# A two-layer graph network: a planner's due times set by pair, and its choice between two kinds of matmul

## Chip, cores, metric

One NeuronCore of one Trainium2 chip runs the whole program. The metric is device time in microseconds of one execution; the kernel before takes 771.95 us (median of three runs, 770.51 to 772.46). TensorE is the matmul engine (PE in profiles, PEld its weight loads), VectorE is DVE, ScalarE is ACT, GpSimd is POOL, SyncE is SP.

## What is computed

128 graphs of 128 nodes with 64 features go through two layers, each with a residual and a layer norm. `x` is (128, 128, 64), `adj` is (128, 128, 128), symmetric in its pattern, about 6% of its entries are nonzero, the diagonal included.

```python
# layer 0
mask = (adj > 0.0)
xj_proj = x @ W1a
diff = x[:, :, None, :] - x[:, None, :, :]
h = relu(xj_proj[:, :, None, :] + diff @ W1b + b1)
hm = einsum('bjkh,bjk->bjh', h, mask)
y = hm @ W2 + deg[..., None] * b2
x = layernorm(x + y)
# layer 1
agg = einsum('bmn,bnd->bmd', adj, x)
h = elu(agg @ V1 + c1)
h = elu(h @ V2 + c2)
x = layernorm(x + h @ V3 + c3)
```

## The kernel before, in words

Two graphs make a pair, and 64 pairs go through a software pipeline. Layer 0 would need a hidden vector for each of 128 x 128 node pairs; the kernel makes one only for edges. Nodes are sorted by degree, each sorted node gets as many slots as its place may need, and the slots of a pair are cut into nine blocks (`BLOCKS`: first node, last node, slots a node). A block is a *unit*. For each unit ScalarE copies the nodes' own part into a PSUM bank (L839), TensorE adds the neighbours' part by 18 matmuls against a one-hot matrix (L851, `oh`), and VectorE sums absolute values over the slots (L860, `sums`). There are four such banks (`edges`, `NE = 4`), so a unit's copy waits for the reduction of the unit four before.

Around the units each pair has these stages, written as generators that yield one step at a time:

- `prepare`: degrees (L532, VectorE), keys (L539, L540, POOL), their spread over the partitions (L545, L547, TensorE), ranks and permutation (L554, L561, VectorE).
- `sort_x` and `project_a`: L574, L578, L582, then L592 (TensorE, three matmuls), the bias copies L599 that make `aj`, `sa` (L606, POOL), L612 and L615, `ea` (L621) and `corr` (L628).
- `sort_mask`: L637, L640 (TensorE), copies L645 and L647, L651 (TensorE), `vp` (L654), and nine one-hot blocks (L661, VectorE).
- `turn` and `project_c`: transposes L676, L677 with copy L681, then L694, L697 (TensorE) and the split of their result into three bf16 parts `cp` (L704, L708, L711, L713).
- `finish`: `hm` (L771, POOL), L776, L780, L783 (TensorE), `ys` (L787), L793 (TensorE), the first norm, L800 and L809 (TensorE), an ELU (`r` L755, `e` L758, `h` L761), L815, a second ELU, L820 and L822, the second norm, the output (L826, an SP DMA).

The matmuls of the units and L578, L612, L615, L800 produce 64 output partitions each, and two of them run in the two column halves of the array (128*64 in the profile); the kernel calls this mode `PE:t`. All others use the full array (128*128; L694 two row halves, 64*128), mode `PE`.

The order on each engine is not written by hand. `Flow` (L88 to L174) plans it while the program is built: a simulated clock for each engine, a list of threads (generators), each with a next step that has an engine, a cost, the events it needs and a due time. `run` finds the step that can start first, then looks at the steps on the same engine that could start within `NEAR` (for TensorE `NEAR_PE`) of it, and takes the one with the lowest rank. The rank is the due time, plus `HOLD` if the step would change TensorE's mode; a change also delays a step by `SWITCH` in the plan. The due times are the tables `DUE`, one figure a step, plus `ROUND` times the pair's number; a unit's is `pace(u)`, and a unit's copy isn't planned before that. A step's result counts as there `LAG` after its planned end. The chip sees only the order; semaphores that follow from it do the rest, and no clock is waited for on the chip. Loads of pair p + 3 start with the first unit of pair p (`AHEAD`).

Of the kernel before, what the change touches and what calls it, by code (L numbers as in the profile page):

```python
# [87 lines left out]
class Flow:  # L88
# [8 lines left out]

    LAG = 0.2
    NEAR = 0.1
    NEAR_PE = 0.03  # L100
    SWITCH = 0.1
    HOLD = 0

    def __init__(self, banks):
        self.clock = {}
# [41 lines left out]
    def _switch(self, engine, mode):  # L147
        return self.SWITCH if engine == "PE" and mode != self.mode else 0.0

    def _rank(self, th):  # L150
        engine, _, mode = th[4][0].partition(":")
        return th[0] + (self.HOLD if self._switch(engine, mode) else 0.0), th[1]

    def run(self):
        while self.threads:
            ready = [(t, th) for t, th in ((self._ready(th[4]), th) for th in self.threads)
                     if t is not None]
            t, th = min(ready, key=lambda r: (r[0], r[1][0], r[1][1]))
            first = th[4][0].split()[0].partition(":")[0]
            near = t + (self.NEAR_PE if first == "PE" else self.NEAR)  # L160
            t, th = min((r for r in ready if r[1][4][0].split()[0].partition(":")[0] == first
                         and r[0] <= near), key=lambda r: self._rank(r[1]))
            engine, cost, after, banks, fn = th[4]
            args = []
            if banks:
                self.free.sort(key=lambda f: f[0])
                args = [self.free.pop(0)[1] for _ in range(banks)]
            fn(*args)
            for e in engine.split():
                e, _, mode = e.partition(":")  # L170
                self.clock[e] = t + cost
                if e == "PE":
                    self.mode = mode
            self._next(th, ([t + cost + self.LAG], *args))  # L174


def sparse(tc, env):
# [4 lines left out]
    LAY, NB = g.LAY, g.NB  # L182
# [6 lines left out]
    EV = {}  # L189


    ROUND = 11.14
    AHEAD = 3
    PACE = ROUND / NB

    DUE = {
        "prepare": (-34.32, -34.43, -29.25, -33.33, -26.26),
        "sort_x": (-25.05, -19.47, -20.79, -15.63, -11.78, -14.33, -11.15, -5.27, -5.97),
        "sort_mask": (-24.98, -24.21, -19.11, -17.63, -31.08, -14.67, -12.13, -9.2, -7.19, -6.42,
                      -4.21, -1.99, -12.24, -7.24),  # L200
        "turn": (-25.52, -21.42),
        "project_c": (-19.53, -25.02, -26.5, -19.03, -18.18, -16.73, -23.86),
        "finish": (7.83, 15.84, 19.72, 16.78, 21.09, 22.6, 28.99, 31.57, 29.07, 31.37, 30.6,
                   34.42, 35.7, 33.91, 37.94, 41.34, 41.72, 43.55, 44, 37.02, 51.36),
        "unit": (-1.1, 0.98, 2.36),
    }

    def pace(u):
        return PACE * u

    def begin_thread(name, p, gen):
        flow.start(ROUND * p, DUE[name], gen)
# [310 lines left out]
    def prepare(p):  # L523

        a = ADJ[p]
        d = S[p] = {}
        mk = d["mk"] = prep.tile([P, 2, N], BF16, name="mk")
        deg = prep.tile([P, 2], F32, name="deg")

        def count():  # L530
            for s in range(2):
                nc.vector.tensor_scalar(mk[:, s, :], a[:, s, :], 0.0, 0.0, op0=OP.is_gt,  # L532
                                        op1=OP.add, accum_out=deg[:, s:s + 1])
        ev, = yield ("DVE", 0.54, [event("load", p)], 0, count)
        degb = prep.tile([P, 2], BF16, name="degb")
        keyc = prep.tile([P, 2], F32, name="keyc")

        def keys():
            nc.gpsimd.tensor_copy(degb, deg)  # L539
            nc.gpsimd.tensor_sub(keyc, deg, jcol)  # L540
        ev, = yield ("POOL PORT", 0.43, [ev] + made("jcol"), 0, keys)

        def spread(key):
            for s in range(2):
                nc.tensor.matmul(key[:, s * N:(s + 1) * N], degb[:, s:s + 1].to_broadcast([P, P]),  # L545
                                 identb, start=True, stop=True)
            nc.tensor.matmul(key[:, 2 * N:3 * N], small, iotb, start=True, stop=True)  # L547
        ev, key = yield ("PE", 0.17, [ev] + made("identb", "small", "iotb"), 1, spread)
        pos = prep.tile([P, 2], F32, name="pos")
        cmp = prep.tile([P, 2, N], BF16, name="cmp", bufs=3)  # L550

        def rank():
            for s in range(2):
                nc.vector.scalar_tensor_tensor(cmp[:, s, :], key[:, s * N:(s + 1) * N],  # L554
                                               keyc[:, s:s + 1], tie, op0=OP.subtract,
                                               op1=OP.is_gt, accum_out=pos[:, s:s + 1])
        ev, = yield ("DVE", 0.54, [ev] + made("tie"), 0, rank)
        permb = d["permb"] = prep.tile([P, 2, N], BF16, name="permb")

        def permute():  # L560
            nc.vector.tensor_tensor(permb, key[:, 2 * N:3 * N].rearrange("p (s n) -> p s n", s=1)  # L561
                                    .to_broadcast([P, 2, N]),
                                    pos.rearrange("p (s o) -> p s o", o=1).to_broadcast([P, 2, N]),
                                    op=OP.is_equal)
        ev, = yield ("DVE", 0.36, [ev], 0, permute)
        flow.give(key, ev)
        begin_thread("sort_x", p, sort_x(p, ev))
        begin_thread("sort_mask", p, sort_mask(p, ev))
# [17 lines left out]
    def project_a(p, xsT, ev):  # L586
# [16 lines left out]
        happened(ev, "aj", p)  # L603
        have = ev
        sa = prep.tile([P, 3, N], F32, name="sa", bufs=3)
        evs, = yield ("POOL PORT", 0.95, [have] + made("srow"), 0, lambda: nc.gpsimd.tensor_mul(sa, aj, srow))  # L606

        def short(eb):

# [60 lines left out]
    def turn(p):  # L670
# [3 lines left out]
        def transpose(t):  # L674
            for s in range(2):
                nc.tensor.transpose(t[:, s * N:(s + 1) * N], a[:, s, :], ident)  # L676
            nc.tensor.transpose(t[:, 2 * N:3 * N], flat(xx), ident)  # L677
        ev, t = yield ("PE", 0.4, [event("load", p)] + made("ident"), 1, transpose)
        turned = d["turned"] = prep.tile([P, 3, N], F32, name="turned", bufs=9)
        ev, = yield ("ACT", act(3 * N), [ev], 0,  # L680
                     lambda: nc.scalar.copy(flat(turned), t[:, :3 * N]))  # L681
# [34 lines left out]
    def norm(yps, ev, name, rest, shift):  # L716
# [15 lines left out]
        def factors():  # L732
            nc.gpsimd.tensor_scalar(ve, st[:, :, 2], 1.0 / F, EPS, op0=OP.mult, op1=OP.add)  # L733
            nc.gpsimd.tensor_tensor(rs, ve, mhalf, op=OP.pow)  # L734
            if shift:
                for s in range(2):
                    nc.gpsimd.tensor_scalar(nb[:, s:s + 1], st[:, s, 1:2], rs[:, s:s + 1], -1.0,  # L737
                                            op0=OP.mult, op1=OP.mult)
        ev, = yield ("POOL PORT", 1.24 if shift else 0.88, [ev] + made("mhalf"), 0, factors)
        o = work.tile([P, 2, F], F32, name=name, bufs=6)  # L740

        def apply():
# [23 lines left out]
    def finish(p):  # L766
# [24 lines left out]
        def unsort(t):  # L791
            for s in range(2):
                nc.tensor.matmul(t[:, s * O:(s + 1) * O], d["permT"][:, s, :],  # L793
                                 ys[:, s * O:(s + 1) * O], start=True, stop=True)
        ev, t = yield ("PE", 0.45, [ev, event("permT", p)], 1, unsort)
        x1, ev = yield from norm(t, ev, "x1", xx, True)

        def aggregate(t):
# [8 lines left out]
        def hidden1(zb):  # L807
            for s in range(2):
                nc.tensor.matmul(zb[:, s * N:(s + 1) * N], v1p[:, s, :], agg,  # L809
                                 start=True, stop=True)  # L810
        ev, zb = yield ("PE", 0.45, [ev] + made("v1p"), 1, hidden1)
        h1, ev = yield from elu(zb, ev, "h1", 0)

        def hidden2(zb):
            nc.tensor.matmul(zb[:, :2 * N], v2s, h1, start=True, stop=True)  # L815
        ev, zb = yield ("PE", 0.44, [ev], 1, hidden2)
        h2, ev = yield from elu(zb, ev, "h2", 1)

        def last(t):
# [300 lines left out]
```

## Time and profile before

| | us |
|---|---|
| median of three runs | 771.95 |
| profiled execution | 770.88 |
| its span, first to last instruction | 769.0 |
| first L851 matmul starts at | 22.8 |
| L851: busy TensorE time, 10368 matmuls | 390.6 |
| L860: busy VectorE time, 576 reductions | 330.2 |
| L839: busy ScalarE time, 576 copies | 309.7 |
| L661: busy VectorE time, 576 blocks | 167.6 |

The clock that TensorE was granted is 0.994 over the span. Busy times are sums over the profiled execution; records of TensorE overlap, since one matmul's end runs beside the next one's start. An fp32 matmul appears as two records. Matmul lines show the array's shape in use behind the tile names (128*64, 128*128, 64*128), then the moving operand. In a timeline, equal instructions that follow each other are one line: start, time from first start to last end, and their number.

### The profile page before, as it was taken

To read this page: it belongs to the slowest core of one execution; us is meant where nothing else is said; L and a number is where in the kernel's file an instruction comes from. 1 tells how busy PE (TensorE), PEld (TensorE's weight loads), DVE (VectorE), ACT (ScalarE), POOL (GpSimd) and SP (SyncE) were. 2 spreads that over 40 slices of the span, in tenths; PEclk is the share of its full clock that TensorE was granted. 3 is DMA by queue.
4 is the path that set the end of the run, shared out by engine and by line. 5 is a ranking of instruction groups with operands and counts; after the bars stand their busy time and mean duration, and the time that the engine had idled before them with its cause. 6 is when DMAs were issued, how large, how long until landed. Compare 5 with 4: busy or idle time off the path is not lost.

```text
span 769.0 us, 35363 instructions
## 1 busy us (share of the span) xinstructions
PE 746.9 (97%) x14487; PEld 671.7 (87%) x14488; DVE 717.1 (93%) x2357; ACT 702.0 (91%) x1990; POOL 432.9 (56%) x806
## 2 busy tenths in 40 slices
PE   7899999999999999999999999999999999999993
PEld 5688998999899899889889889989899889989992
DVE  7999999999999999999999999999999999999982
ACT  5788999999999999999999999999999999999974
POOL 6445565665665665655555555556566566566542
PEclk9999999999999999999999999999999999999997
DMA  3011110110111011011011011011011011100000
GB/s 81 3 24 26 27 30 21 27 31 20 27 30 27 21 30 30 16 31 30 18 30 31 17 30 30 21 27 30 21 27 30 21 27 30 27 20 21 10 9 18
DMA packets 63881, 19.75 MB, mean 26 GB/s; under 512 B 46816, under 2 KB 63712, under 8 KB 63712
## 3 DMA queue, kind: packets, MB, share of 16 engines
q1 hardware_dynamic: 63008, 17.12, 9.6%
q8 instruction: 115, 1.88, 1.1%
q14 instruction: 54, 0.44, 0.2%
q10 hardware_dynamic: 704, 0.30, 0.2%
HBM read 13.14 MB, written 4.19 MB: 23 GB/s over the span
## 4 chain that ended last, share of the span: by engine, by line
PE 93%; DVE 3%; ACT 1%; DMA 1%; issue 1%; POOL 0%; ACTq 0%; DVEq 0%
PE e L851 44%; PE m L592 6%; PE m L776 5%; PE m L694 5%; PE m L809 4%; PE m L815 4%; PE m L822 4%; PE m L793 3%; PE m L578 2%; PE m L676 2%; PE m L800 2%; PE m L637 2%; PE m L651 2%; PE m L780 1%; PE m L697 1%; DVE sums L860 1%
## 5 line engine op out<-in xcount | busy, mean ns | idle before, releaser
L851 PE MATMUL e<-oh,cp 128*64 128x162 bf16 (+3 forms) x10368 | 390.6, 228 | 1.8 <-ACT e L839 1.5
L851 PEld LDWEIGHTS <-cp 128*64 128x64 bf16 x10368 | 356.8, 110 | 30.6 <-issue 22.6
L860 DVE TENSOR_REDUCE sums<-e 128x54 f32<-128x486 f32 (+8 forms) x576 | 330.2, 608 | 12.8 <-PE e L851 12.4
L839 ACT COPY e<-aj 128x504 f32<-128x504 f32 (+6 forms) x576 | 309.7, 558 | 7.2 <-DVE sums L860 6.7
L661 DVE TENSOR_TENSOR oh<-vp,slotc 128x336 bf16<-128x336 bf16 (+6 forms) x576 | 167.6, 319 | 1.8 <-PE e L851 1.7
L606 POOL TENSOR_TENSOR sa<-aj,srow 128x384 f32<-128x384 f32 x64 | 65.3, 1020 | 121.6 <-ACT aj L599 118.8
L733 POOL TENSOR_SCALAR ve<-st 128x2 f32<-128x2 f32 x128 | 24.5, 191 | 156.1 <-DVE st L726 150.5
L734 POOL TENSOR_TENSOR rs<-ve,mhalf 128x2 f32<-128x2 f32 x128 | 88.9, 695 | 10.6
L713 POOL TENSOR_TENSOR cp<-r,cp 128x512 bf16<-128x512 f32 x64 | 74.2, 1159 | 13.2 <-ACT cp L711 13.2
L771 POOL TENSOR_TENSOR hm<-sums,corr 128x384 f32<-128x384 f32 x64 | 64.0, 1000 | 11.8 <-DVE sums L860 11.8
L755 ACT ACTIVATE r<-m,cc 128x256 f32<-128x256 f32 x128 | 64.3, 502 | 4.1 <-PE m L809 3.1
L628 POOL TENSOR_TENSOR corr<-ea,sa 128x384 f32<-128x384 f32 x64 | 64.1, 1001 | 0.9 <-DVE ea L621 0.7
L761 DVE SCALAR_TENSOR_TENSOR h<-m,cc,e 128x256 f32<-128x256 f32 x128 | 60.7, 475 | 3.7 <-ACT e L758 3.7
L592 PE MATMUL m<-xsT,wad 128*128 128x128 f32 x384 | 58.3, 288 | 0.8 <-DVE r L708 0.6
L599 ACT ACTIVATE aj<-m,b1c 128x128 f32<-128x128 f32 x192 | 57.0, 375 | 1.0 <-PE m L592 1.0
L744 ACT ACTIVATE x<-y,nb,rs 128x64 f32<-128x64 f32 x128 | 49.4, 434 | 9.3 <-POOL nb L737 9.2
L758 ACT ACTIVATE e<-r 128x256 f32<-128x256 f32 x128 | 57.6, 451 | 0.1
L554 DVE SCALAR_TENSOR_TENSOR cmp<-m,keyc,tie 128x128 bf16<-128x128 f32 x128 | 39.9, 349 | 16.3 <-PE m L547 15.4
L776 PE MATMUL m<-w2d,hm 128*128 128x128 f32 x384 | 53.9, 277 | 0.3 <-POOL hm L771 0.3
L708 DVE TENSOR_TENSOR r<-m,cp 128x256 f32<-128x256 f32 x128 | 52.2, 411 | 0.8 <-ACT cp L704 0.7
L776 PEld LDWEIGHTS m<-w2d,hm 128*128 128x128 f32 x384 | 48.6, 193 | 1.0 <-POOL hm L771 0.5
L592 PEld LDWEIGHTS m<-xsT,wad 128*128 128x128 f32 x384 | 47.7, 191 | 1.8 <-DVE r L708 0.8
(145 smaller groups left out, 1346.8 us busy)
## 6 DMA issues: line engine op xcount, KB each, us to landing
adj<-in_adj_dram SPq DMA_DIRECT2D x64, 128.0 KB, 2.4
xx<-in_x_dram SPq DMA_DIRECT2D x64, 64.0 KB, 2.3
out_dram<-o SPq DMA_DIRECT2D x64, 64.0 KB, 1.7
degs<-ys SPq DMA_DIRECT2D x64, 1.0 KB, 1.7
w1s<-in_L_gnn_W_dram ACTq DMA_DIRECT2D x2, 96.0 KB, 3.1
w2s<-in_L_gnn_W_dram ACTq DMA_DIRECT2D x2, 48.0 KB, 2.8
v2s<-in_L_gnn_W_dram SPq DMA_DIRECT2D x1, 64.0 KB, 3.0
v1d<-in_L_gnn_W_dram SPq DMA_DIRECT2D x2, 32.0 KB, 2.0
```

The lines of the kernel that those rows point to most:

```text
L592: nc.tensor.matmul(aps[:, c * N:(c + 1) * N], wad[:, c, :], xsT, start=True, stop=True)
L606: evs, = yield ("POOL PORT", 0.95, [have] + made("srow"), 0, lambda: nc.gpsimd.tensor_mul(sa, aj, srow))
L628: ev, = yield ("POOL PORT", 1.05, [ev, evs], 0, lambda: nc.gpsimd.tensor_sub(corr, ea, sa))
L661: lambda: nc.vector.tensor_tensor(oh[:, :, c].rearrange("p b (s w) -> p b s w", w=w), vp[:, :, p0:p1].rearrange("p b (o w) -> p b o w", o= ...
L713: lambda: nc.gpsimd.tensor_sub(cp[:, 2], r1, cp[:, 1]))
L734: nc.gpsimd.tensor_tensor(rs, ve, mhalf, op=OP.pow)
L755: lambda: nc.scalar.activation(r, z, AF.Relu, bias=c, scale=-1.0))
L771: lambda: nc.gpsimd.tensor_sub(hm, d["sums"], d["corr"]))
L776: nc.tensor.matmul(yb[:, :2 * O], hm[:, c, :], flat(w2d[:, c]), start=(c == 0), stop=False)
L839: lambda: nc.scalar.copy(e.rearrange("p (c s w) -> p c s w", c=3, w=w), d["aj"][:, :, p0:p1].rearrange("p c (o w) -> p c o w", o=1) .to_br ...
L851: nc.tensor.matmul(e[s * HB:(s + 1) * HB, c * n:(c + 1) * n], cp[:, k, s, c * HB:(c + 1) * HB], oh[:, s, base:base + n], start=False, stop ...
L860: nc.vector.tensor_reduce(d["sums"][:, :, p0:p1], e.rearrange("p (c s w) -> p c w s", c=3, w=w), AX.X, OP.add, apply_absolute_value=True)
```

## The change

No tile, matmul, copy or DMA is changed; the diff is to what the planner is told.

- `NEAR_PE` goes from 0.03 to 0.05. A new `STAY` of 0.1 lets a TensorE step of the mode now in use be chosen if it could start within 0.1 of the earliest. `HOLD` goes from 0 to 9.1, so among the steps in reach one that changes the mode ranks as if due 9.1 us later.
- `ROUND` goes from 11.14 to 10.91. A unit's `pace` was spread evenly, `ROUND / 9` apart; it is now `ROUND` times the pair plus 0.59 times the unit's number, so the nine are due within 4.7 us of their pair's start.
- All tables of `DUE` are new. Preparing steps are due later than before (the first of `prepare` at -21.43 instead of -34.32), finishing steps earlier (the last used ones around 20 instead of 37 to 51).
- Planned costs of seven steps change by 0.03 to 0.11 either way.

```diff
@@ -97,9 +97,10 @@
 
     LAG = 0.2
     NEAR = 0.1
-    NEAR_PE = 0.03
+    NEAR_PE = 0.05
     SWITCH = 0.1
-    HOLD = 0
+    STAY = 0.1
+    HOLD = 9.1
 
     def __init__(self, banks):
         self.clock = {}
@@ -147,6 +148,9 @@
     def _switch(self, engine, mode):
         return self.SWITCH if engine == "PE" and mode != self.mode else 0.0
 
+    def _same(self, th):
+        return th[4][0].split()[0].partition(":")[2] == self.mode
+
     def _rank(self, th):
         engine, _, mode = th[4][0].partition(":")
         return th[0] + (self.HOLD if self._switch(engine, mode) else 0.0), th[1]
@@ -158,8 +162,11 @@
             t, th = min(ready, key=lambda r: (r[0], r[1][0], r[1][1]))
             first = th[4][0].split()[0].partition(":")[0]
             near = t + (self.NEAR_PE if first == "PE" else self.NEAR)
+
+            stay = t + self.STAY if first == "PE" else near
             t, th = min((r for r in ready if r[1][4][0].split()[0].partition(":")[0] == first
-                         and r[0] <= near), key=lambda r: self._rank(r[1]))
+                         and (r[0] <= near or r[0] <= stay and self._same(r[1]))),
+                        key=lambda r: self._rank(r[1]))
             engine, cost, after, banks, fn = th[4]
             args = []
             if banks:
@@ -189,24 +196,24 @@
     EV = {}
 
 
-    ROUND = 11.14
+    ROUND = 10.91
     AHEAD = 3
-    PACE = ROUND / NB
+    UNIT = 0.59
 
     DUE = {
-        "prepare": (-34.32, -34.43, -29.25, -33.33, -26.26),
-        "sort_x": (-25.05, -19.47, -20.79, -15.63, -11.78, -14.33, -11.15, -5.27, -5.97),
-        "sort_mask": (-24.98, -24.21, -19.11, -17.63, -31.08, -14.67, -12.13, -9.2, -7.19, -6.42,
-                      -4.21, -1.99, -12.24, -7.24),
-        "turn": (-25.52, -21.42),
-        "project_c": (-19.53, -25.02, -26.5, -19.03, -18.18, -16.73, -23.86),
-        "finish": (7.83, 15.84, 19.72, 16.78, 21.09, 22.6, 28.99, 31.57, 29.07, 31.37, 30.6,
-                   34.42, 35.7, 33.91, 37.94, 41.34, 41.72, 43.55, 44, 37.02, 51.36),
-        "unit": (-1.1, 0.98, 2.36),
+        "prepare": (-21.43, -22.36, -22.69, -20.72, -21.04),
+        "sort_x": (-15.03, -12.06, -13.19, -6.77, -6.47, -11.28, -12.01, 0.14, 0.41),
+        "sort_mask": (-12.71, -9.98, -12.21, -12.26, -12.11, -7.07, -6.36, -6.41, -5.45, -4.29,
+                      -4.35, -3.8, -3.8, -4.28),
+        "turn": (-16.08, -7.32),
+        "project_c": (-14.14, -13.31, -10.75, -12.7, -10.78, -6.83, -12.64),
+        "finish": (-0.94, 6.84, 5.02, 8.44, 9.21, 9.24, 8.9, 10.51, 16.67, 19.63, 14.77, 10.14,
+                   15.75, 12.69, 17.93, 20.46, 19.2, 19.6, 23.98, 19.96, 19.4, 20.24, 21.31),
+        "unit": (1.9, 2.36, 3.81),
     }
 
     def pace(u):
-        return PACE * u
+        return ROUND * (u // NB) + UNIT * (u % NB)
 
     def begin_thread(name, p, gen):
         flow.start(ROUND * p, DUE[name], gen)
@@ -538,7 +545,7 @@
         def keys():
             nc.gpsimd.tensor_copy(degb, deg)
             nc.gpsimd.tensor_sub(keyc, deg, jcol)
-        ev, = yield ("POOL PORT", 0.43, [ev] + made("jcol"), 0, keys)
+        ev, = yield ("POOL PORT", 0.32, [ev] + made("jcol"), 0, keys)
 
         def spread(key):
             for s in range(2):
@@ -603,7 +610,7 @@
         happened(ev, "aj", p)
         have = ev
         sa = prep.tile([P, 3, N], F32, name="sa", bufs=3)
-        evs, = yield ("POOL PORT", 0.95, [have] + made("srow"), 0, lambda: nc.gpsimd.tensor_mul(sa, aj, srow))
+        evs, = yield ("POOL PORT", 1.0, [have] + made("srow"), 0, lambda: nc.gpsimd.tensor_mul(sa, aj, srow))
 
         def short(eb):
 
@@ -675,7 +682,7 @@
             for s in range(2):
                 nc.tensor.transpose(t[:, s * N:(s + 1) * N], a[:, s, :], ident)
             nc.tensor.transpose(t[:, 2 * N:3 * N], flat(xx), ident)
-        ev, t = yield ("PE", 0.4, [event("load", p)] + made("ident"), 1, transpose)
+        ev, t = yield ("PE", 0.33, [event("load", p)] + made("ident"), 1, transpose)
         turned = d["turned"] = prep.tile([P, 3, N], F32, name="turned", bufs=9)
         ev, = yield ("ACT", act(3 * N), [ev], 0,
                      lambda: nc.scalar.copy(flat(turned), t[:, :3 * N]))
@@ -736,7 +743,7 @@
                 for s in range(2):
                     nc.gpsimd.tensor_scalar(nb[:, s:s + 1], st[:, s, 1:2], rs[:, s:s + 1], -1.0,
                                             op0=OP.mult, op1=OP.mult)
-        ev, = yield ("POOL PORT", 1.24 if shift else 0.88, [ev] + made("mhalf"), 0, factors)
+        ev, = yield ("POOL PORT", 1.27 if shift else 0.97, [ev] + made("mhalf"), 0, factors)
         o = work.tile([P, 2, F], F32, name=name, bufs=6)
 
         def apply():
@@ -792,7 +799,7 @@
             for s in range(2):
                 nc.tensor.matmul(t[:, s * O:(s + 1) * O], d["permT"][:, s, :],
                                  ys[:, s * O:(s + 1) * O], start=True, stop=True)
-        ev, t = yield ("PE", 0.45, [ev, event("permT", p)], 1, unsort)
+        ev, t = yield ("PE", 0.4, [ev, event("permT", p)], 1, unsort)
         x1, ev = yield from norm(t, ev, "x1", xx, True)
 
         def aggregate(t):
@@ -808,12 +815,12 @@
             for s in range(2):
                 nc.tensor.matmul(zb[:, s * N:(s + 1) * N], v1p[:, s, :], agg,
                                  start=True, stop=True)
-        ev, zb = yield ("PE", 0.45, [ev] + made("v1p"), 1, hidden1)
+        ev, zb = yield ("PE", 0.49, [ev] + made("v1p"), 1, hidden1)
         h1, ev = yield from elu(zb, ev, "h1", 0)
 
         def hidden2(zb):
             nc.tensor.matmul(zb[:, :2 * N], v2s, h1, start=True, stop=True)
-        ev, zb = yield ("PE", 0.44, [ev], 1, hidden2)
+        ev, zb = yield ("PE", 0.48, [ev], 1, hidden2)
         h2, ev = yield from elu(zb, ev, "h2", 1)
 
         def last(t):
```

## Prediction

> **What bounds the kernel now.** I read the shares of busy time first, then the busy time of the engines in single rounds (a round is one pair of graphs: nine units plus all other stages of one pair each), then the waits, then TensorE's own timeline inside a round.
>
> ```profile
> PE 746.9 (97%) x14487; PEld 671.7 (87%) x14488; DVE 717.1 (93%) x2357; ACT 702.0 (91%) x1990; POOL 432.9 (56%) x806
> PE 93%; DVE 3%; ACT 1%; DMA 1%; issue 1%; POOL 0%; ACTq 0%; DVEq 0%
> ```
>
> TensorE is the chain that ended last for 93% of the span. A busy TensorE is not yet a bound, so the rounds have to confirm it; columns are stretch, then length, then PE, PEld, DVE, ACT and POOL busy, then clock and DMA:
>
> ```profile
> 22.80:34.00 11.20, 10.27 (x234) 8.68 (x234) 10.51 (x31) 8.60 (x24) 4.30 (x4) 1.00 0.01 2
> 300.00:311.43 11.43, 11.43 (x230) 10.38 (x230) 10.96 (x37) 10.90 (x32) 6.62 (x12) 1.00 0.11 27
> 500.00:511.43 11.43, 11.43 (x228) 10.37 (x227) 10.96 (x37) 10.89 (x33) 6.62 (x12) 1.00 0.11 26
> 746.10:769.00 22.90, 9.98 (x77) 7.60 (x71) 7.98 (x24) 9.07 (x27) 7.30 (x17) 0.80 0.07 15
> ```
>
> The timeline repeats every 11.43 us, and in such a round TensorE is busy throughout, VectorE 10.96 and ScalarE 10.90. The view of TensorE's waits between 100 and 700 us is empty: no matmul there waits for another engine. So a round costs what its matmuls cost one after the other, and VectorE and ScalarE have about half a microsecond left. In the last 22.9 us TensorE works less than half the time: there the end of the last pair is a chain of latencies.
>
> What is inside TensorE's 11.43 us is seen where its array changes between column halves (128*64, units and L578, L612, L615, L800) and the full array (128*128). The start of a group minus the start of the one before is what that one cost:
>
> ```profile
> 302.36 0.50 PE L851 MATMUL e<-oh,cp 128*64 128x154 bf16 x9
> ...
> 302.78 0.28 PE L651 MATMUL m<-mtp,prefix 128*128 128x256 bf16 x1
> 302.90 0.83 PE L776 MATMUL m<-w2d,hm 128*128 128x128 f32 x6
> 303.57 0.34 PE L780 MATMUL m<-cp,mtp 128*128 128x64 bf16 x6
> ...
> 305.44 0.50 PE L809 MATMUL m<-agg,v1p 128*128 128x128 f32 x3
> 305.87 0.34 PE L851 MATMUL e<-oh,cp 128*64 128x170 bf16 x4
> ...
> 309.33 0.61 PE L822 MATMUL m<-v3s,h 128*128 128x64 f32 x4
> 309.87 0.70 PE L694 MATMUL m<-wc,turned 64*128 64x256 f32 x4
> ...
> 732.07 0.61 PE L822 MATMUL m<-v3s,h 128*128 128x64 f32 x4
> 732.52 0.89 PE L776 MATMUL m<-w2d,hm 128*128 128x128 f32 x6
> 733.24 0.34 PE L780 MATMUL m<-cp,mtp 128*128 128x64 bf16 x6
> ```
>
> Six L776 records take 303.57 - 302.90 = 0.67, 0.112 each. Three L809 records of the same shape, up to a unit, take 305.87 - 305.44 = 0.43 instead of 0.336: 0.09 more. The other way, nine unit records before L651 take 0.42, while unit records of this size run at 36 in 1.28 (299.89 to 301.17), 0.32 for nine: 0.10 more. L822 before L694, which uses row halves, takes 0.54 for four records; the same four before L776, where the shape stays, take 732.52 - 732.07 = 0.45, so 0.09 more. So each change of the array's shape costs about 0.10 us, in either direction and for a shape the planner does not distinguish.
>
> **What the skill says.** The Trainium skill, "TensorEngine Tiling (Array Packing)", Key Properties: "Changing tiling mode (not just tile) drains the TensorE." It gives no price; the trace agrees and gives 0.09 to 0.10. "TensorE: Matmul & The Clock Gate", Weight-path perf modes: fast weight load is not on for fp32 weights. The trace agrees: L776's fp32 records load for 193 ns (PEld row) and L822's 64-column records still cost 0.11 each (0.45 for four), as much as 128 columns; so an fp32 group that follows a very short matmul pays for its first load (L592, behind the one-column L783, takes 304.55 - 303.80 = 0.75 for six, 0.08 over L776). The same page, Part 2: only TensorE's loads are pulled ahead, its matmuls stay in program order. So the order as built is the order that runs.
>
> **The change, part by part.**
>
> 1. No instruction of computation is added, removed or resized. Due times, costs and the three constants are read only by the planner, so the effect is the new order, and the waits that follow from it.
>
> 2. Changes of shape. From the built order I counted, between full-array and column-half work: before, 278 in all, and from round 7 on exactly four in each round (two full-size runs per pair). After, 382 in all, and from round 7 to 61, 55 rounds, six in each: units 154, 170, 162 / L809, L651 / units 66, 168 / L776 to L783, L815, L694, L697, L793 / units 112, 168, 154, 169 / L820, L822, L592, L676, L677, L637, L640, L545, L547. The short run L809 + L651, about half a microsecond of work, stands alone. So the new order has three full-size runs per pair where the old one has two, whatever HOLD is meant to do. L694's own two changes to row halves stay inside a full-size run in both. Startup has ten fewer (33 for 43), the end four more; the sum is +104. At 0.105 each (0.09 to 0.10 measured at the boundary, plus about 0.02 because the first unit behind a change starts slower: the 170-unit takes 305.87 to 306.55, 0.68, for 0.66 at the pace of the units behind it, in half of the changes): +10.9 us. Bounds 104 x 0.09 = +9.4 and 104 x 0.12 = +12.5.
>
> 3. First fp32 loads. Before, a round pays L592 behind L783 0.08, L809 behind the 64-column L793 0.05 and L815 behind L547 about 0.05 (0.58 for two double-width records, less 0.45 and the change's 0.09): 0.18. After, L815 stands behind L783 (0.08), L793 behind the 64-column bf16 L697 (0.05), and L592 behind L822 (0.05: at 732.52 the six L776 behind L822 take 0.72, against 0.67). L809 and L776 now open full-size runs, which only bf16 groups do before; the end shows what an fp32 group pays there: L793 behind a unit takes 0.50 for four (731.02 to 731.52), 0.05 over L822's 0.45. With 0.05 each the new sum is 0.28. Net +0.10 a round, times 55: +5.5 us, bounds 0 and +10.
>
> 4. Start and end. Work is also moved across the ends. Before, behind the last unit stand six L809, eight L822, three L815 and four L793 instructions; after, four, six, two and two. One pair's worth of each, about 0.45 us a group, hence 1.8 us, ran in an end in which TensorE idles and now runs in rounds that it bounds: +1.8. Ahead of the first unit two pairs' L592 (1.5 us) and some L637, L651 and L545 are gone (0.7): the first unit may start about two microseconds sooner, and the work comes back in the early rounds; in the stretches from 22.8 to 34 us TensorE idles 0.9, so part is absorbed, but less prepared work also means early units that wait. I take +1 for it, bounds -3 (all early idling filled) and +6. The latency chain of the last pair, from its last unit to its output, is the same operations: 0.
>
> 5. Waits in a round. Every engine queue was reordered and the planner now sets more semaphore waits (290 more instructions that only wait, some three a round on TensorE, one each on VectorE and POOL). In the trace such a wait on TensorE takes 0.05 in its queue ahead of the array (not in its busy time), with matmuls running: 0, unless what it waits for is late. The tightest of the new places is L815 behind L809: unit 66, its reduction on VectorE, the two L532 counts, h (L761), then L815. From the unit's start: unit 0.28, matmul end 0.19, reduction 0.35, counts 2 x 0.28 overlapping to 0.41, h 0.47, some 0.05 of signalling: 1.75. TensorE has in the meantime unit 66 0.28, unit 168 0.66, a change 0.10, L776 to L783 0.90: 1.94. It fits by 0.2. The first-layer ELU itself, L809 end 0.19, r 0.51, e 0.46, h 0.47 with 0.15 of signalling: 1.8, against 0.25 + 1.94. It fits too. If such a chain is 0.1 to 0.3 later than I add up, it costs that in each round; it is the upper rival below.
>
> 6. POOL, DMA and SP: the same instructions. POOL is busy 6.62 of 11.43; loads still start three pairs ahead. Planner costs for L541, L606, L739 (0.32, 1.0, 1.27/0.97) move starts, not durations. Nothing is late there by half a round.
>
> Sum: +10.9 + 5.5 + 1.8 + 1 = +19.2. The profiled execution took 770.88, its span 769.0 and 1.9 around it, which nothing here changes: 790.1. The runs' median, 771.95, lies 1.1 higher, so 790 to 791; I forecast 790. A round should be 11.43 + 0.21 + 0.10, about 11.74.
>
> **Rivals.**
>
> A. As above: 790, own range 782 to 798 (parts at their lower and upper bounds, not all at once). Chance 0.73.
>
> B. The new order also brings in-order waits (VectorE's chain in front of L815, or ScalarE copies ahead of ys and L793): +0.1 to 0.2 in 55 rounds on top, 5.5 to 11, hence about 799. For it: 0.2 of slack only, VectorE at 96%. Against: the longer round itself gives VectorE and ScalarE 0.3 more. Chance 0.19.
>
> C. The other sign: the 0.10 at the boundaries is not a drain but a wait on data that the view does not show (the first unit waits for ScalarE's copy, L651 and L637 for VectorE's results). Then shorter, more frequent runs would let data arrive: TensorE would lose the four stalls, 0.4 a round, and come to VectorE's 10.96 at best: 55 x 0.40 = -22, about 750; with half of it gone, 761. It decides from the point at which more than half of the stalls are data. Against it: the excess is 0.09 to 0.10 at every one of the boundaries, L694's included, where nothing new is awaited on leaving. Chance 0.05.
>
> D. The added changes are hidden since other engines hold the round anyhow: 772. Against: the empty view of waits. Chance 0.03.
>
> **Range and chances.** Some 0.3%, 2.3 us, is what a measurement of this kernel can tell from no change. A and B together hold 0.92; from 781 (A's low end with a smoother start) to 801 (just above B's middle) some 0.85 lie. Faster by more than 0.3%: C, 0.05; within: D, 0.02; slower: 0.93.
>
> **What would show it.** Right: rounds of about 11.74 with TensorE busy throughout, three full-size runs a round, each boundary 0.09 to 0.10 over its neighbours, VectorE and ScalarE unchanged in busy time and idler in share. Wrong: L815 or L793 appearing in TensorE's waits (B), rounds at 11.43 or below (D, C), or L809 after a unit starting without its 0.10.

## The result, and the profile after

The changed kernel takes 802.23 us (median of four runs, 802.06 to 803.04), the kernel before 771.28 (median of four, 770.51 to 772.46): a ratio of 1.040, 95% interval 1.037 to 1.043. The forecast was 790 with a range of 781 to 801: the right sign, 12 us too little, and the range missed by 1.2. The profiled span went from 769.0 to 800.5, +31.5.

All line numbers of the changed kernel are 7 higher than before's: L858 are the units (L851), L816 is L809, L783 is L776, L822 is L815, L701 is L694, L800 is L793, L658 is L651. The page of after, shares of busy time and the chain that ended last:

```profile
PE 774.4 (97%) x14487; PEld 672.7 (84%) x14488; DVE 727.7 (91%) x2357; ACT 703.5 (88%) x1990; POOL 440.1 (55%) x806
PE 91%; DVE 3%; ACT 2%; SPq 1%; DMA 1%; issue 1%; POOL 1%; ACTq 0%; POOLq 0%; DVEq 0%
```

TensorE is the bound as before, with the same 14487 matmuls and 27.5 us more busy time. Busy time in stretches of after (stretch, length, then PE, PEld, DVE, ACT, POOL, granted clock and DMA): the first seven rounds, one steady round, and what is behind the start of the last unit's last matmul.

```profile
18.70:105.30 86.60, 79.50 (x1524) 68.74 (x1524) 78.46 (x255) 70.26 (x194) 42.49 (x73) 1.00 0.08 19
...
424.00:435.85 11.85, 11.85 (x230) 10.37 (x228) 11.19 (x36) 10.91 (x32) 6.75 (x13) 1.00 0.11 26
...
776.60:800.50 23.90, 9.30 (x62) 6.53 (x57) 6.04 (x19) 6.60 (x19) 5.04 (x11) 0.68 0.06 13
```

The same view of before, its first seven rounds:

```profile
22.80:100.90 78.10, 75.08 (x1504) 65.98 (x1505) 74.44 (x237) 67.09 (x185) 39.38 (x65) 1.00 0.09 21
```

A steady round is 11.85 us and TensorE is busy in all of it; VectorE is busy 0.2 more than before and still 0.7 below TensorE; ScalarE is as before. The view of TensorE's waits between 130 and 700 us is empty in after, too; that alone proves little, since it lists only stretches in which the engine idles (in two_runs below it is empty while a unit waits in every round). Rounds counted from 0, each from the start of its 162-wide unit to that of the next, the 31.5 us divide so:

| part | before | after | difference |
|---|---|---|---|
| to the first 162-wide unit | 22.76 | 18.67 | -4.1 |
| rounds 0 to 6 | 78.10 | 86.63 | +8.5 |
| rounds 7 to 60, 54 rounds | 617.4 | 640.2 | +22.8 |
| rounds 61 and 62 | 20.36 | 22.85 | +2.5 |
| from the last round's first unit to the end | 30.4 | 32.1 | +1.7 |

So 22.8 us come from 0.42 more in each steady round, and 8.6 from start and end. Where a round's 0.42 sits is seen in the timeline of TensorE in after (start, time from first start to last end, instruction, count):

```profile
401.77 0.79 PE L858 MATMUL e<-oh,cp 128*64 128x162 bf16 x17
402.49 0.71 PE L816 MATMUL m<-agg,v1p 128*128 128x128 f32 x4
403.04 0.27 PE L658 MATMUL m<-mtp,prefix 128*128 128x256 bf16 x1
403.24 1.14 PE L858 MATMUL e<-oh,cp 128*64 128x66 bf16 x36
404.31 0.94 PE L783 MATMUL m<-w2d,hm 128*128 128x128 f32 x6
405.08 0.34 PE L787 MATMUL m<-cp,mtp 128*128 128x64 bf16 x6
405.26 0.19 PE L790 MATMUL m<-onesb,mtp 128*128 128x1 bf16 x2
405.31 0.68 PE L822 MATMUL m<-h,v2s 128*128 128x256 f32 x2
405.92 0.70 PE L701 MATMUL m<-wc,turned 64*128 64x256 f32 x4
406.55 0.23 PE L704 MATMUL m<-b2p,onesb 128*128 128x64 bf16 x2
406.62 0.64 PE L800 MATMUL m<-ys,permT 128*128 128x64 f32 x4
407.19 2.60 PE L858 MATMUL e<-oh,cp 128*64 128x112 bf16 x72
```

Three full-size runs a round, as forecast, the first of them only L816 and L658. L783's six records take 405.08 - 404.31 = 0.77 where before's L776 took 0.67: 0.10 more, and L816's four take 0.55, where 0.45 is what four such records take behind another full-size group. Both groups now open a full-size run. In single records, the first of each group takes 0.213 instead of 0.112. That is over and above the change of shape, whose cost stands with its neighbours: L658 before a unit 0.20 instead of 0.12, and 0.16 instead of some 0.06 from the last unit record to L783's first. Taken record by record over a round, the first records of the fp32 groups are 0.23 longer than before's in sum (L783 0.10, L800 0.08, L816 0.05, L822 0.03, L599 -0.03) and the records at changes of shape 0.19; the two make up the 0.42, so nothing is left for a wait.

### The profile page after: what moved, and what is told of

Its sections match the earlier page's. It is cut to its first block, busy times and chain, and to the rows that moved or that the text cites. A ratio compares the mean times of both kernels' runs of the same rounds, so it can differ in the third digit from the quotient of the medians.

```text
span 800.5 us, 35653 instructions
## 1 busy us (share of the span) xinstructions
PE 774.4 (97%) x14487; PEld 672.7 (84%) x14488; DVE 727.7 (91%) x2357; ACT 703.5 (88%) x1990; POOL 440.1 (55%) x806
## 4 chain that ended last, share of the span: by engine, by line
PE 91%; DVE 3%; ACT 2%; SPq 1%; DMA 1%; issue 1%; POOL 1%; ACTq 0%; POOLq 0%; DVEq 0%
PE e L858 44%; PE m L783 7%; PE m L599 6%; PE m L816 5%; PE m L701 5%; PE m L822 4%; PE m L800 4%; PE m L829 3%; PE m L807 2%; PE m L585 2%; PE m L683 2%; PE m L787 1%; DVE sums L867 1%; PE m L704 1%; PE m L827 1%; DVE oh L668 1%
## 5 line engine op out<-in xcount | busy, mean ns | idle before, releaser
L858 PE MATMUL e<-oh,cp 128*64 128x162 bf16 (+3 forms) x10368 | 393.3, 228 | 5.3 <-ACT e L846 3.0
L858 PEld LDWEIGHTS <-cp 128*64 128x64 bf16 x10368 | 346.2, 110 | 32.0 <-issue 20.5
L846 ACT COPY e<-aj 128x504 f32<-128x504 f32 (+6 forms) x576 | 298.2, 553 | 8.5 <-DVE sums L867 8.3
L668 DVE TENSOR_TENSOR oh<-vp,slotc 128x336 bf16<-128x336 bf16 (+6 forms) x576 | 162.6, 327 | 5.0 <-PE e L858 4.9
L778 POOL TENSOR_TENSOR hm<-sums,corr 128x384 f32<-128x384 f32 x64 | 68.7, 1073 | 60.5 <-DVE sums L867 60.5
L718 ACT CAST cp<-r 128x512 bf16<-128x512 f32 x64 | 39.6, 619 | 52.8 <-DVE r L715 52.8
L762 ACT ACTIVATE r<-m,cc 128x256 f32<-128x256 f32 x128 | 61.7, 482 | 5.5 <-PE m L822 2.7
L783 PE MATMUL m<-w2d,hm 128*128 128x128 f32 x384 | 59.4, 291 | 0.7 <-POOL hm L778 0.7
L599 PE MATMUL m<-xsT,wad 128*128 128x128 f32 x384 | 56.8, 284 | 0.0
L783 PEld LDWEIGHTS m<-w2d,hm 128*128 128x128 f32 x384 | 47.7, 191 | 8.2 <-POOL hm L778 0.9
L765 ACT ACTIVATE e<-r 128x256 f32<-128x256 f32 x128 | 54.3, 424 | 0.2
```

Of the source, the lines that this page charges most:

```text
L599: nc.tensor.matmul(aps[:, c * N:(c + 1) * N], wad[:, c, :], xsT, start=True, stop=True)
L668: lambda: nc.vector.tensor_tensor(oh[:, :, c].rearrange("p b (s w) -> p b s w", w=w), vp[:, :, p0:p1].rearrange("p b (o w) -> p b o w", o= ...
L762: lambda: nc.scalar.activation(r, z, AF.Relu, bias=c, scale=-1.0))
L778: lambda: nc.gpsimd.tensor_sub(hm, d["sums"], d["corr"]))
L783: nc.tensor.matmul(yb[:, :2 * O], hm[:, c, :], flat(w2d[:, c]), start=(c == 0), stop=False)
L846: lambda: nc.scalar.copy(e.rearrange("p (c s w) -> p c s w", c=3, w=w), d["aj"][:, :, p0:p1].rearrange("p c (o w) -> p c o w", o=1) .to_br ...
```

## The experiments

Three kinds: matmuls added to before (prices), the planner's rule alone, and orders replayed from a list. In the last kind `Flow.run` doesn't choose; a list names the thread whose step is emitted next (`ORDER` stands here for that list, which the file holds packed). Steps, tiles and instructions stay, and only their order differs:

```diff
     def run(self):
-        while self.threads:
...
+        for key in ORDER:
+            th = next(r for r in self.threads if self._key(r) == key)
+            t = self._ready(th[4])
             engine, cost, after, banks, fn = th[4]
```

**What a change of shape and an fp32 opening cost.** Ahead of each pair's 66-slot unit a matmul of 128 columns is added to before: as two column halves (`p_half`, no change of shape), as one full-size bf16 matmul (`p_full`, two changes more), as one full-size fp32 matmul (`p_f32`, which also opens the full-size run). The added matmul is no part of the layer, and with it those units' sums no longer hold: most likely they lack what ScalarE had copied into the unit's bank. The three kernels serve as prices alone.

In p_half:

```diff
+            if i == 1:
+                for s in range(2):
+                    nc.tensor.matmul(edges[u % NE][s * HB:(s + 1) * HB, 256:384], onesb[:, :HB],
+                                     onesb[:, :P], start=True, stop=True, skip_group_check=True)
```

in p_full (and with `ident, ident` for the two operands in p_f32):

```diff
+            if i == 1:
+                nc.tensor.matmul(edges[u % NE][:, 256:384], onesb[:, :P], onesb[:, P:],
+                                 start=True, stop=True, skip_group_check=True)
```

> The kernel before, its order unchanged, with two bf16 matmuls of 128 columns in the two column halves (the units' own shape) put ahead of each pair's 66-slot unit, into columns of its bank that the unit doesn't use. Both theories: no change of shape is added, so a round grows by the one 128-column stream, 0.056 us: 64 x 0.056 = +3.6, about 775.

> The same place, but one full-array bf16 matmul of 128 columns in place of the two halves, so that each round has two more changes of shape (six for four), and nothing else waits. If a change of shape costs 0.10 to 0.11 whatever stands there: 64 x (0.056 + 0.21) = +17, about 788. If what stands at the boundaries of the kernel before is a wait on data: as the halves, about 775.

> The same place, one full-array fp32 matmul of 128 columns (0.224 us as two records), opening and closing a full-size run by itself. If an fp32 group that opens a full-size run pays 0.10 on its first record on top of the change: 64 x (0.224 + 0.21 + 0.10) = +34, about 805. If 0.05, as predicted: about 802. If nothing: about 799. The first record tells: 0.213 between starts, or 0.112 to 0.165.

Measured: 776.53 (ratio 1.0048, 1.0031 to 1.0066), 788.29 (1.0229, 1.0193 to 1.0264) and 806.45 us (1.0450, 1.0422 to 1.0478). Steady rounds are 11.49, 11.715 and 11.97, for before's 11.43. TensorE's timeline, the added matmul and the unit behind it, in p_half:

```profile
400.93 0.22 PE L850 MATMUL e<-onesb 128*64 128x128 bf16 x2
400.99 0.45 PE L855 MATMUL e<-oh,cp 128*64 128x66 bf16 x18
```

in p_full:

```profile
406.84 0.23 PE L849 MATMUL e<-onesb 128*128 128x128 bf16 x1
407.00 0.47 PE L854 MATMUL e<-oh,cp 128*64 128x66 bf16 x18
```

and in p_f32:

```profile
406.04 0.49 PE L849 MATMUL e<-ident 128*128 128x128 f32 x2
406.45 0.47 PE L854 MATMUL e<-oh,cp 128*64 128x66 bf16 x18
```

p_full less p_half is 0.225 a round for two changes: 0.11 each, with the start of the next unit included. From start to start the added matmul takes 0.06, 0.16 and 0.41. The fp32 one has two records, which run at 0.112 each where nothing holds them (0.224, against 0.056 for the bf16 one): 0.168 of the 0.26 between p_full and p_f32. The other 0.09 is what an fp32 group pays for opening a full-size run, beside the change itself. My forecast had 0.05.

**The same in the changed kernel.** L651 (bf16) is moved ahead of L809 in rounds 8 to 61 of the changed order, so that a bf16 matmul opens this run; six changes stay.

```text
order of the changed kernel:  unit 162 | L809 L651 | unit 66
l651_first:                   unit 162 | L651 L809 | unit 66
```

> The changed kernel's order, replayed from a list, with L651 moved ahead of L809 in rounds 8 to 61, so that a bf16 matmul of 256 columns opens the short run instead of an fp32 group; six changes a round as in the changed kernel. If an fp32 group that opens a run pays 0.10 on its first record: -0.10 in 54 rounds, -5.4, about 797, and L809's four records take 0.45 instead of 0.55. If L809's slow first record is a wait for agg: unchanged, about 802.

Measured: 797.22 us (ratio to before 1.0332, 1.0312 to 1.0353), 5.0 less than the changed kernel's 802.23; a round is 11.77 for 11.855. Its timeline (126 lines lower than before: L777 is L651, L935 is L809):

```profile
410.64 0.82 PE L977 MATMUL e<-oh,cp 128*64 128x162 bf16 x18
411.39 0.28 PE L777 MATMUL m<-mtp,prefix 128*128 128x256 bf16 x1
411.51 0.61 PE L935 MATMUL m<-agg,v1p 128*128 128x128 f32 x4
412.05 0.62 PE L977 MATMUL e<-oh,cp 128*64 128x66 bf16 x22
```

L777 opens at no extra price (0.12 to the next start), and L935's group is 0.54 to the unit, 0.45 and a change. An exchange of two neighbours takes away 0.09 a round, so the opening price is a matter of which group comes first, not of the number of changes. By itself this run doesn't exclude a wait for `agg`: L651 takes 0.12 ahead of L809, which would hide such a wait as well. p_f32 does exclude it: its added matmul reads only the constant `ident`, and its first record takes the same 0.213.

**Two full-size runs again.** In 50 rounds of the changed order L651 and L809 are put ahead of L776 and L815 at the run's end, with the copies, `ys` and ELU steps moved along: four changes a round.

```text
changed kernel:  | L809 L651 | units | L776 L780 L783 L815 L694 L697 L793 | units | L820 ... L547 |
two_runs:        | L651 L809 L776 L780 L783 L694 L697 L793 L815 | units | L820 ... L547 |
```

> The changed kernel's order replayed from a list, with L651 and L809 moved to open the second full-size run (ahead of L776) and L815 to its end in 50 rounds, so that a round has two full-size runs and four changes of shape, and L809 is not opened by a change. Theory (changes and openings set the round): two changes less, 2 x 0.11, and two fp32 openings less, 2 x 0.10, so 0.42 a round, 21 us in 50 rounds: from 802 to about 781, a round of 11.43. Rival (data waits take the place of the changes: L793 comes nearer to the ys that it reads, units nearer to their one-hot blocks): the round stays at about 11.8 and the time at about 800; TensorE's waits then name L793 or the units. Each 0.1 us of such waits a round takes 5 us of the gain.

Measured: 792.02 us (1.0266, 1.0250 to 1.0283), 10.2 less than the changed kernel, half of the theory's 21; a round is 11.63. Both openings went (L776's six records 0.67, L809's four 0.45). What came in their place is in the timeline of all engines; the number in brackets is idle time before:

```profile
420.22 0.33 DVE L787 TENSOR_TENSOR oh<-vp,slotc 128x308 bf16<-128x308 bf16 x1
...
420.31 0.24 PE L741 MATMUL m<-mtp,mtwo 128*64 128x128 bf16 x2
420.31 0.13 PEld L977 LDWEIGHTS <-cp 128*64 128x64 bf16 x2
420.39 1.01 PE L977 MATMUL e<-oh,cp 128*64 128x162 bf16 x19
...
420.61 0.70 PEld L977 LDWEIGHTS <-cp 128*64 128x64 bf16 x19 [0.16 <-issue]
```

The unit's first matmul starts at 420.39, its second at 420.61; in between the weight loads stop for 0.16. The view names no releaser, but the semaphores in the trace do: the second matmul waits on one that VectorE counts up, and in each of the 13 rounds from 152 to 293 us it starts 0.04 behind the count of this one-hot block (L787, which ends at 420.22 + 0.33 = 420.55). The block isn't the unit's own: its 308 columns belong to a unit of 154 slots, while the 162-slot unit reads a block of 324, finished by 412.66. So the unit waits for more than its data; why the wait reaches so far was not tried. It is the rival's kind of wait, at a unit and not at L793. Another 0.07 stands where L694's change to row halves now follows the one-column L783 (L783's two take 0.12 instead of 0.05). Sum: about -0.42 + 0.17 + 0.07 = -0.18, measured -0.22.

**The rule alone, and the tables alone.** `rule_alone` is before with the new constants; `hold_back` is the changed kernel with the old ones. The constants of rule_alone, against before (hold_back has the reverse, with STAY at 0; `run` has the changed kernel's choice in both):

```diff
-    NEAR_PE = 0.03
+    NEAR_PE = 0.05
-    HOLD = 0
+    STAY = 0.1
+    HOLD = 9.1
```

> The kernel before with the new rule alone (HOLD 9.1, STAY 0.1, NEAR_PE 0.05), old due times and pace. Its built order keeps four changes a round. If only the order counts: rounds of 11.43 and 772 to 777, the start being other. If the rule itself brings waits: 785 or more.

> The changed kernel with HOLD 0, STAY 0 and NEAR_PE 0.03, as before, and the new due times and pace kept. Its built order has the same six changes of shape a round from round 7 on. If the due times and the pace make the short run, not the rule of choice: about 802, within 4 for another start. If the rule makes it: toward 772.

Measured: rule_alone 780.81 us (1.0111, 1.0085 to 1.0137), hold_back 804.45 (1.0427, 1.0403 to 1.0451). A steady round each, of rule_alone

```profile
400.00:411.43 11.43, 11.43 (x232) 10.38 (x228) 10.96 (x37) 10.90 (x32) 6.64 (x12) 1.00 0.11 24
```

and of hold_back

```profile
300.00:311.86 11.86, 11.86 (x227) 10.37 (x226) 11.18 (x36) 10.91 (x33) 6.75 (x12) 1.00 0.10 24
```

The old tables give the old round under either rule, the new tables the new one. So the six changes come from the tables (due times, `ROUND`, `pace` and planned costs together; which of them was not tried), and the constants that should keep TensorE in its shape neither prevent nor cause them. The miss is rule_alone's time: it needs 18 rounds, of up to 13.8 us, before the order settles, and in the profiled execution the last unit's last matmul starts 8.7 us later than before (754.8 for 746.1), of which up to 1.7 can come from 3.4 us at half the clock (18.8 to 22.2).

**The start.** The changed order up to round 9, from the tenth round on before's order with its rounds and its end; 278 changes in all.

```text
after_start:  changed order until the first unit of round 10 | what is left, in before's order
```

> The changed kernel's order up to its tenth round (start and early rounds), from there on the order of before with its rounds and its end, replayed from a list; 278 changes in all, as before. Theory (the changed kernel's early rounds idle TensorE, units waiting for copies and one-hot blocks, and this isn't made up for later): some 4 us from the start, three early rounds with 0.42 more each, 1.3, and 1 to 2 where the orders are joined: 777 to 779. Rival (the start's idle time is made up for, the earlier first unit being worth as much): 772 to 773, and the excess of the changed kernel's start and end lies in its end alone.

Measured: 784.25 us (1.0164, 1.0147 to 1.0181), 6 more than expected. Its first seven rounds take 86.3 us (86.6 in the changed kernel, 78.1 before), as expected; from the thirteenth on nearly all rounds are 11.43 or 11.44. But the join, three rounds from the tenth on, costs 7.0. A window around the join and the end of after_start:

```profile
129.00:170.20 41.20, 37.22 (x687) 32.62 (x683) 36.24 (x112) 33.99 (x97) 20.17 (x32) 0.96 0.09 21
759.00:783.90 24.90, 12.11 (x75) 9.09 (x69) 7.90 (x24) 9.22 (x27) 7.33 (x17) 0.67 0.07 14
```

TensorE idles 4.0 us at the join and is busy 2.9 more there than in three of before's rounds (37.2 for 34.3). Up to 1.3 of the 2.9 can come from a stretch of 3.4 us at half the clock (146.5 to 149.9, busy 2.55); the rest fits before's order, which prepares pairs further ahead. Another 2.0 stand behind the last unit (24.9 for 22.9), at a lower clock. So this run repeats the slow early rounds, but doesn't tell cleanly what the start alone is worth in the whole: the join mixes in.

**A better order.** If first fp32 loads have a price, before can be improved at the same four changes. `b_592` moves L592 behind the transposes L676 and L677; `b_s3` also puts L793 behind L809 and exchanges some units of a run.

```text
before:  | L651 L776 L780 L783 L592 L676 L677 L793 L809 | units
b_592:   | L651 L776 L780 L783 L676 L677 L592 L793 L809 | units
b_s3:    | L651 L776 L780 L783 L676 L677 L592 L809 L793 | units
```

> The order of before replayed from a list, with L592 moved behind the two transposes L676 and L677 (51 pairs), so that its fp32 group no longer follows the one-column L783; four changes a round as before. Theory (an fp32 group's first load behind a very short matmul costs 0.05 to 0.08): 2.5 to 4 us less than before, about 768.5. Rival (that excess belongs to L783 itself and stays with whatever follows it, or L592 pays the same behind L677): no difference from before.

> The order of before replayed from a list, with L592 behind L676 and L677, L793 behind L809 (fp32 behind fp32 of the full width, so that L809 no longer follows the 64-column L793) and some units of a run exchanged with each other; four changes a round. Theory (first fp32 loads cost 0.05 to 0.08 each where they follow a short matmul): two of them less, 0.10 to 0.13 a round in about 52 rounds, 5 to 7 us, against some tenths lost where the new order sets in: about 766. Rival (the price of a first load moves along, here to L809 behind L592 and L793 behind L809; or exchanged units wait for their copies): no difference from before, or a microsecond or two more.

Measured: b_592 769.85 us (0.9975, 0.9961 to 0.9988), b_s3 764.71 (0.9912, 0.9898 to 0.9926), before 770.99. Rounds are 11.39 and 11.31. The timeline of b_s3 (122 lines lower: L798 is L676, L714 is L592, L931 is L809, L915 is L793):

```profile
405.11 0.19 PE L905 MATMUL m<-onesb,mtp 128*128 128x1 bf16 x2
405.16 0.42 PE L798 MATMUL m<-ident,adj 128*128 128x128 f32 x2
405.42 0.27 PE L799 MATMUL m<-ident,xx 128*128 128x128 f32 x1
405.53 0.83 PE L714 MATMUL m<-xsT,wad 128*128 128x128 f32 x6
406.20 0.61 PE L931 MATMUL m<-agg,v1p 128*128 128x128 f32 x4
406.64 0.56 PE L915 MATMUL m<-ys,permT 128*128 128x64 f32 x4
407.13 1.14 PE L973 MATMUL e<-oh,cp 128*64 128x170 bf16 x36
```

L714 takes 0.67 for before's 0.75. L798 pays part of it: 0.26 where it took 0.22. So b_592's gain, 0.04 a round, is about half of L592's 0.08, since L676 is itself an fp32 transpose; the price of following a very short matmul moves to what comes next, but is smaller for it. In 51 rounds that is 2.2 us; the medians differ by 1.1 only. Outside the rounds executions differ: in b_592's profile 3.4 us ahead of its first unit run at half the clock (from 20.7), in before's none between 12.4 and 759.9. L931 and L915 together take 0.93 for before's 0.99 (0.39 and 0.59). These two edits are -0.10; the remaining 0.02 of b_s3's gain a round lies in the units' order and was not tried apart. b_s3 beats both kernels: 0.9% less than before, 4.7% less than the changed one.

## Why the prediction was right in its sign and missed in size

The profiled sum, in us; the forecast of step 2 is spread over the parts at 0.105 a change, the ten changes fewer at the start and the end's more included.

| term | forecast | measured |
|---|---|---|
| step 2, changes of shape, rounds 7 to 60 | 54 x 0.21 = 11.3 | 54 x 0.22 = 11.9 |
| step 3, first fp32 loads, the same rounds | 54 x 0.10 = 5.4 | 54 x 0.20 = 10.8 |
| step 4, start, to the beginning of round 7 | 1.0 - 1.0 = 0 | 4.4 |
| steps 2 to 4, rounds 61 and 62 | 2.5 | 2.5 |
| step 4, behind them | 0 | 1.7 |

- *Step 1*, only the order changes: right; the same instructions, and all of the excess in rounds is TensorE's own time.
- *Step 2*, two more changes a round at 0.105: right. Six changes a round in after, and 0.11 each in p_full against p_half. The Trainium skill, "TensorEngine Tiling (Array Packing)", Key Properties, says that a change of mode drains TensorE; the traces agree in so far as each change costs 0.10 to 0.11.
- *Step 3* is the term of the round that failed, in size: "L809 and L776 now open full-size runs, which only bf16 groups do before; the end shows what an fp32 group pays there: L793 behind a unit takes 0.50 for four (731.02 to 731.52), 0.05 over L822's 0.45." Two readings in it are wrong. L793 is compared with another group; behind a full-size fp32 group L793 itself takes 0.39 for four, so it paid 0.11 for opening (0.10 by its first record). And outside the steady rounds fp32 groups of 128 columns do open full-size runs in before: L776 behind a unit at 50.53, 58.38 and 725.18, with 0.77 each for 0.67.

```profile
50.53 0.94 PE L776 MATMUL m<-w2d,hm 128*128 128x128 f32 x6
51.30 0.34 PE L780 MATMUL m<-cp,mtp 128*128 128x64 bf16 x6
...
304.88 0.56 PE L793 MATMUL m<-ys,permT 128*128 128x64 f32 x4
305.27 0.66 PE L809 MATMUL m<-agg,v1p 128*128 128x128 f32 x4
...
731.02 0.66 PE L793 MATMUL m<-ys,permT 128*128 128x64 f32 x4
731.52 0.66 PE L809 MATMUL m<-agg,v1p 128*128 128x128 f32 x4
```

 So the price of 0.10 stood in the trace of before. Both openings of after pay it (0.213 instead of 0.112 in the first record; 0.09 in p_f32 and in l651_first), and L793 behind L697, put at 0.05, pays 0.08. The net is 0.20 a round (0.42 less 0.22 for changes; 0.23 record by record) for 0.10, 5.4 us more. The bound that I gave for this term, +10, is about where it fell. The mechanism holds: it is a first load that nothing hides. In a steady round of before L776's first weight load starts 0.11 ahead of its first matmul (302.79 for 302.90), beside L651; where L776 opens a run the two start together. A change of shape isn't needed for it: at 748.29 L776 stands behind L822, in the same shape, after 0.34 of idle time, and pays the same 0.10.

```profile
50.53 0.74 PEld L776 LDWEIGHTS m<-w2d,hm 128*128 128x128 f32 x6
...
302.79 0.76 PEld L776 LDWEIGHTS m<-w2d,hm 128*128 128x128 f32 x6
...
748.29 0.94 PE L776 MATMUL m<-w2d,hm 128*128 128x128 f32 x6 [0.34 <-POOL hm L771]
749.07 0.34 PE L780 MATMUL m<-cp,mtp 128*128 128x64 bf16 x6
```

- *Step 4* failed at the start, also in size: "I take +1 for it, bounds -3 (all early idling filled) and +6." The first 162-wide unit comes 4.1 sooner, but the seven rounds behind it take 8.5 more. Of these, 4.4 are busy time (79.5 for 75.1), which the sooner start about pays for; some 1.9 of it is work of other stages that before did elsewhere, an estimate from the groups' number and their times in a steady round. The other 4.1 are idle time, 7.1 for 3.0, and this is what the +1 had too small. TensorE's waits up to 106 us in after name most of the cause,

```profile
PE e L858 <- ACT e L846: 3.0, 8, 0.9
PE e L858 <- DVE oh L668: 1.7, 5, 0.4
```

 for before's

```profile
PE e L851 <- ACT e L839: 1.3, 2, 1.1
```

 (who waits, on what, us in total, times, longest). Units due close together wait for ScalarE's copies and VectorE's one-hot blocks before enough lies ready. That cause is read from the trace; the run that should have isolated it (after_start) repeated these rounds, but its join hid their net.
- *The end*: rounds 61 and 62 took the 2.5 of the forecast, but by luck. The forecast put work there that left the end. By the count of records, what these rounds hold more is preparing work, one pair's L592, L612, L615, L651, L676, L677, L694 and L697; of what left the end, a pair's L800 and L815 and two pairs' L820 and L822 stand in rounds 0 to 6. Of the 1.7 behind, 0.7 stand ahead of the last unit's last matmul and 1.0 behind it (23.9 for 22.9), at a lower granted clock (0.68 for 0.80). after_start, with before's end, takes 24.9 there at 0.67: so at the same clock the end of after is about 1.0 shorter, which step 4 had at 0, and the clock costs about 2.0 (last section).
- *Steps 5 and 6*, no waits in a round, nothing from POOL or DMA: right. L815's chain fits, and changes and first records make up the whole 0.42.
- *The rivals*: B named a time near the result (799) by a mechanism that isn't there: no wait in the steady rounds. A wait of its kind, on VectorE, appears in two_runs. C and D fell with rounds above 11.43.

The range missed because the bounds of three terms were held not to fall on the same side at once; two fell high together (first fp32 loads and the start), and the end added 1.7.

## What to carry to other kernels

Where one engine is busy throughout, a new order of the same work is priced by its boundaries: count the changes of shape per round in the order as built, then look at which group stands first behind each change and let a bf16 group stand there, not an fp32 one. Take such a price from the same group in two places, search the start and the end for such places as well as the steady rounds, or measure it with one added matmul. Sum the early rounds of a new plan too: to the beginning of round 7 they cost 4.4 of the 31.5 us here, and start and end together 8.6. An empty view of waits doesn't show that nothing waits; a round whose excess is placed record by record does.

## What the runs showed of the hardware that was not expected

- An fp32 group that opens a full-size run behind column-half matmuls pays 0.09 to 0.10 us in its first record, on top of the change of shape (0.11). A bf16 matmul in its place pays the change alone. L776 pays the same 0.10 without a change of shape after 0.34 us of idle time.
- Behind the last unit TensorE idles more than half of the time, and the clock granted there differs between executions of one and the same program: before's executions with a mean clock of 0.994 have spans of 768.3 to 769.2 us, those with 0.989 some 770.8 to 772.2. In the profiles the clock falls to half 12.8 to 15.8 us behind the last unit's last matmul in before, p_full, b_592 and b_s3, and 7.7 to 9.1 us behind it in p_half, p_f32, rule_alone, after_start, hold_back, l651_first, two_runs and after. after_start and before end in the same order, in 24.9 us at 0.67 and in 22.9 at 0.80. Some 2 of the 31.5 us can be this. What sets it was not tried; the order may have a part in it, since all 17 executions of after, l651_first, two_runs and hold_back had a mean clock of 0.986 to 0.991, and 20 of before's 43 had 0.994 or more.
